# Rank-9 term carried as nine rows of a gathered list, and x loaded in place, in a two-layer graph kernel

## The chip, the cores and the metric

The kernel runs on one core of a Trainium2 chip. The metric is device time in microseconds (us) of one execution; lower is better. Times of several plain executions are given as their median, and one more execution was taken under the hardware profiler, which also records what every engine and every DMA queue did. Engines are named as in the profile: PE (TensorE matmul), PEld (its weight load), DVE (VectorE), ACT (ScalarE), POOL (GpSimd) and SP (SyncE, which here only issues DMAs).

## The reference, cut to what matters

x is (8, 2048, 128): 8 batches, 2048 nodes, 128 features. adj is a sparse symmetric-pattern 2048 x 2048 matrix in dense storage, with a full diagonal and about 18,400 entries that are not zero.

```
# layer 0
res = si[:, :, None] + sj[:, None, :] + adj * w_r + g_b      # si = x @ w_i, sj = x @ w_j
x   = layernorm(x + (res @ x) @ weight + bias)
# layer 1, five matrices of features: X, two hops of adj, and the same two again
h1  = adj^T X ;  h2 = 2 * adj^T h1 - X
x   = layernorm(x + relu([X, h1, h2, h1, h2] @ Theta1 + bias1))
```

With Y0 = x @ weight, layer 0 is `w_r * adj @ Y0` plus a term that is the same low-rank product for every node: si times the column sums of Y0, plus a row that doesn't depend on the node. For the 8 batches together this is 8 scalars per node (si) and a constant one, against 9 rows of 1024 numbers. This is the rank-9 term.

## The kernel before, in words

**Tiling.** The 2048 nodes are 16 chunks of 128. A chunk of rows is a tile of 128 partitions x 1024 (8 batches x 128 features), 512 KB in fp32. A result chunk is accumulated in two PSUM banks, one per half of the batches ("both halves", `h` in 0 and 1).

**Layer 0, dense and listed chunks.** While adj and x are read (lines 326 to 346 and 688 to 703), Y0 of every chunk is computed into the tile `Y`. Result chunks 0 to 3 are computed densely: their transposed rows of adj stay in `at4`, and `full_rows` multiplies them with all 16 chunks of `Y`. Chunks 4 to 15 are computed from lists: `Y` is stored to `y0_d` in DRAM, and the rows that a chunk needs are gathered back by indirect DMAs, issued from POOL. A listed chunk takes seven gathers (`get_rows`): four lists "T", each for a group of 32 columns, two lists "H", each for 64 columns, and a third list of H for rows that touch both halves of 64 columns. Each list has up to 128 rows, one per partition. The matching coefficients stand in `rct` (three blocks of 128 columns for each chunk, `W` = 384); `get_job` gathers them into `st` and `keep_job` masks them and writes them to `rct`. `listed` multiplies coefficients with gathered rows. The 128 x 128 block on the diagonal is done by `own_rows`, whose Y0 rows are loaded by `own0` on SP's queue (chunks 4 to 7 still lie in `Y`; 8 to 15 are loaded from `y0_d` to `ring`), with a 64 KB block `rd`.

**The rank-9 term.** `si_t(c)` transposes the 37 columns of `si` for a chunk (5 for each half, 32 apart) into PSUM and ACT copies them to `sit`. `rank9(c)` multiplies them with `ub`, 5 rows for each half, in two matmuls with 5 rows of weights. This is done for every chunk, the listed ones too.

**Order of the work.** Each engine runs its instructions in the order in which the program writes them (`Tied`). The loop over listed chunks (lines 839 to 862) issues for each chunk: the gathers on POOL, one job of coefficients, `own_rows`, the own load of chunk c+2, `rank9`, `si_t` of the next chunk, the listed matmuls, `z_add` (adds x), `make_u` of chunk c-2 (transpose of the normalised rows to `x1t`, a product with theta, and a store to `u_d`), the load of x for chunk c+2, and `layernorm`. Gathered rows go round through 12 buffers, chunks 0 to 3 and 8 to 15 of `Y`. x waits in three slots of `ring` and in `spare` (two thirds of `trp`).

**Layer 1.** `hop(1)` and `hop(2)` use the same lists with adj itself (`rc`), gathering from `u_d` and `y_d`. `hop(1)` gathers T rows once chunks 0 to 13 of `u_d` are stored, and H rows once all are.

**Ahead of the loop.** On the way there (lines 777 to 836) `make_ub` builds `ub`, DVE finds the second lists in eight rounds (`rounds2`), `lists_end(1)` turns them into indices after two small matmuls, and chunks 0 to 3 are finished. A path for inputs whose lists are too long (line 962) isn't run for this input.

Of the kernel before, what the change touches and what calls it, by code (L numbers as in the profile page):

```python
# [8 lines left out]
F32 = mybir.dt.float32  # L9
I32 = mybir.dt.int32  # L10
AF = mybir.ActivationFunctionType
ALU = mybir.AluOpType
# [6 lines left out]
def kernel(  # L19
# [34 lines left out]
    HC = NT // 2 + NC  # L54
    NI = NT + HC
    PAD = 40000
    W = 3 * P
    T_ORDER = list(range(6, NC)) + [4, 5]
    NP = LR + NC - LT
# [39 lines left out]
    def flat(t):  # L99
        return t.rearrange("p b f -> p (b f)")  # L100
# [28 lines left out]
    dve.memset(epst, EPS)  # L129
    ones = const.tile([P, P], F32)  # L130
    dve.memset(ones, 1.0)
    e5 = const.tile([1, 5], F32)
    dve.memset(e5, 0.0)
    dve.memset(e5[:, 4:5], 1.0)
    sel = const.tile([P, 8], F32)
    dve.tensor_add(sel, ident[:, 0:8], ident[:, 32:40])
    dve.tensor_add(sel, sel, ident[:, 64:72])
    dve.tensor_add(sel, sel, ident[:, 96:104])
    sel5 = const.tile([P, 4, 5], F32)
    dve.memset(sel5, 0.0)  # L140
    for i in range(4):
        dve.tensor_copy(sel5[:, i, i:i + 1], sel[:, 0:1])
        dve.tensor_copy(sel5[:, i, 4:5], sel[:, 1 + i:2 + i])
    numi = const.tile([P, NC], I32)
    pool.iota(numi, pattern=[[P, NC]], base=1, channel_multiplier=1)
    num = const.tile([P, NC], F32)
    dve.tensor_copy(num, numi)
    coli = const.tile([P, NI], I32)
    pool.iota(coli[:, 0:NT], pattern=[[1, NC], [0, QT]], base=0, channel_multiplier=0)
    pool.iota(coli[:, NT:NT + 2 * NC], pattern=[[1, NC], [0, 2]], base=0, channel_multiplier=0)  # L150
# [9 lines left out]
    idr = const.tile([P, NI], I32)  # L160
    has = const.tile([P, NI], F32)
    over = const.tile([1, 1], I32)
    si = const.tile([P, NC, 37], F32)
    dve.memset(si, 0.0)
    for h in range(2):
        dve.memset(si[:, :, 32 * h + 4:32 * h + 5], 1.0)
    sraw = const.tile([P, NC, B, 2], F32)
    s1 = const.tile([P, NC, 2, 8], F32)
    dve.memset(s1, 0.0)
# [41 lines left out]
            sp.dma_start(out=rr_d[c - ND][:, 1, :], in_=adj[:, c * P:(c + 1) * P])  # L211

    def load_z(c):
        zs[c] = load_x(c, [ring[:, 3], ring[:, 4], ring[:, 5], spare][(c - 2) % 4])

    def pump():
        while todo:
# [67 lines left out]
    def s_rows(c0):  # L285
        c4 = slice(c0, c0 + 4)
        act.activation(
            s1[:, c4, :, 1:5], sraw[:, c4, :, 0].rearrange("p c (h i) -> p c h i", h=2),
            AF.Identity, bias=gb,
        )  # L290
        for h in range(2):
            act.copy(si[:, c4, 32 * h:32 * h + 4], sraw[:, c4, h * HB:(h + 1) * HB, 1])

    pcs = bank[4:6]

# [9 lines left out]
                    tile_position=(0, 32 * j),  # L305
                )

    LAST = list(range(ND)) + list(range(8, NC)) + list(range(4, 8))
    js_first = [X_ORDER[0]] * 2 + [LAST[0]] * (ND - 2)

    def full_rows(c, accs, js):
# [156 lines left out]
    def lists_end(part):  # L468
        b = bank[6 + part]
        if part == 0:  # L470
            lo, hi = 0, NT
            for r in range(2):
                pe.matmul(
                    b[64 * r:64 * r + 64, 0:NT], lists, ident[:, 64 * r:64 * r + 64], start=True,
                    stop=True, skip_group_check=True, tile_position=(0, 64 * r),
                )
        else:
            lo, hi = NT, NI
            for r in range(2):
# [66 lines left out]
    def keep_job():  # L546
        what, c = jobs[kept[0]]
        s = staged(kept[0])
        kept[0] += 1
        m = 2 if c >= ND else 1  # L550
        hc = has[:, columns(c, what)[0]:columns(c, what)[0] + QT]
        for k in range(m):
            if m == 1 or k == 1:
                to = rc[:, c * W:(c + 1) * W]
            else:
                to = rct[:, (c - ND) * W:(c - ND + 1) * W]
            of = s[:, k * P:]
            if what == "T":
                if m == 2:
                    dve.tensor_mul(  # L560
                        to[:, 0:P].rearrange("p (t f) -> p t f", t=QT),
                        strided(of, QT, m * P + TW, TW), hc[:, :, None].to_broadcast([P, QT, TW]),
                    )
                    continue
                for t in range(QT):
                    at = t * (P + TW)
                    dve.tensor_scalar(
                        to[:, TW * t:TW * t + TW], of[:, at:at + TW], hc[:, t:t + 1], None,
                        op0=ALU.mult,
                    )  # L570
# [12 lines left out]
    def make_ub():  # L583
        cs = [trp[:, h].rearrange("p i f -> p (i f)") for h in range(2)]
        for h in range(2):
            act.copy(cs[h], pcs[h])
        pu = bank[4]
        for h in range(2):
            pe.matmul(
                pu[32 * h:32 * h + 5], e5, b0row.rearrange("p i f -> p (i f)"), start=True,  # L590
                stop=False, skip_group_check=True, tile_position=(0, 32 * h),
            )
        for i in range(4):
            s = slice(i * P, (i + 1) * P)
            for h in range(2):
                pe.matmul(
                    pu[32 * h:32 * h + 5, s], sel5[:, i, :], cs[h][:, s], start=False, stop=(i == 3),
                    skip_group_check=True, tile_position=(0, 32 * h),
                )
# [7 lines left out]
    def si_t(c):  # L607
        b = bank[turns[turn[0] % len(turns)]][0:37, 0:P]
        turn[0] += 1
        pe.transpose(b, si[:, c, :], ident)  # L610
        sits[c] = small.tile([37, P], F32, name=f"sit{c}", tag="sit")
        act.copy(sits[c], b)

    def rank9(c, accs):
        sit = sits.pop(c)
        for h in range(2):
            pe.matmul(
                accs[h], sit[32 * h:32 * h + 5], ub[32 * h:32 * h + 5].rearrange("p i f -> p (i f)"),
                start=False, stop=(c < ND), skip_group_check=True, tile_position=(32 * h, 0),
            )  # L620

    def z_add(accs, xr):
# [172 lines left out]
    rounds2([7])  # L795
# [43 lines left out]
    for c in range(ND, NC):  # L839
# [9 lines left out]
        own_rows(0, c, accs, True)  # L849
        if c + 2 < NC:  # L850
            own0(c + 2)
        rank9(c, accs)
        if c + 1 < NC:
            si_t(c + 1)
        listed(0, c, accs, "T")
        listed(0, c, accs, "H")
        z_add(accs, zs[c])
        for n in [c - 2] if c < 14 else [12, 13] if c == 14 else [14]:
            make_u(n, zs[n], x1t[n], u_of[n])
        if c + 2 < NC:  # L860
            load_z(c + 2)
        layernorm(zs[c], f"0_{c}")


# [170 lines left out]
```

## Time and profile before

| what | value |
|---|---|
| median of 3 executions (lowest, highest) | 850.22 us (850.05, 854.02) |
| the profiled execution, whole / its span | 818.08 us / 816.3 us |
| mean granted TensorE clock | 0.971 |
| PE busy / DVE / ACT / POOL | 732.8 / 394.7 / 192.7 / 445.2 us |
| gathers of Y0 and second-hop rows, 196 | 212.0 us of POOL, 1081 ns each |
| gathers of first-hop rows, 112 | 111.8 us of POOL |
| gathers of coefficients to `st`, 84 | 90.3 us of POOL |
| rank-9 matmuls, 64 records | 20.1 us of PE |
| transposes of `si`, 16 | 4.7 us of PE |
| own Y0 and second-hop rows to `ring`, 11 loads of 512 KB on SP | median 23.2 us from issue to landing |

The profile gives, for each group of instructions, busy time, the mean of one in nanoseconds, and what ended the idle time ahead of it. One fp32 matmul shows as two records. "DMA share" is the mean busy share of the 16 DMA engines. A line number in the profile is that of a helper here (L72) for nearly all instructions, so groups are told apart by tile names: `bank<-ub,sit` is the rank-9 term, `bank<-ident,si` its transpose, `Y<-y_d,idx` a gather of rows (the profile writes y_d for `y0_d` too), `st<-rr_d,idx` a gather of coefficients, `ring<-y_d` an own load. SPq lines are the issue of a DMA on SP's queue.

### The profile page before, as it was taken

The numbers are of one execution on the slowest core, as the hardware profiler recorded it, in microseconds if no ns is written. First come the engines' busy times: TensorE is split into PE (matmuls) and PEld (weight loads), VectorE is DVE, ScalarE is ACT, GpSimd is POOL, SyncE is SP. The second block draws the span as 40 slices with busy tenths as digits, with TensorE's granted clock in tenths as the row PEclk, the third lists the DMA queues.
The fourth block names the chain that finished last, engine by engine and source line by source line (L and its number), as shares of the span: only waits on it lengthen the run. The fifth ranks groups of instructions, "written<-read, shape, count | busy, mean of one in ns | idle before, by whom it ended". The sixth has DMA issues, their size and how long they took to land.

```text
span 816.3 us, 10067 instructions
## 1 busy us (share of the span) xinstructions
PE 732.8 (90%) x3554; PEld 364.9 (45%) x3554; DVE 394.7 (48%) x591; ACT 192.7 (24%) x439; POOL 445.2 (55%) x432
## 2 busy tenths in 40 slices
PE   4999999997999998988798888898899999999992
PEld 4666566642644343434345243333344454444441
DVE  4664876578341655555533000000100377777775
ACT  3757554321200332313222000000000011111101
POOL 1000000477747876776344677776774777776740
PEclk9999999997999999999899899999999999999997
DMA  8999999999326799999969799899999799999982
GB/s 264 296 314 316 352 292 295 314 398 347 119 89 223 244 346 368 341 344 367 356 224 344 246 364 360 314 365 346 339 372 357 252 343 357 370 385 389 363 299 68
DMA packets 165299, 253.90 MB, mean 311 GB/s; under 512 B 17255, under 2 KB 118020, under 8 KB 163192
## 3 DMA queue, kind: packets, MB, share of 16 engines
q0 software_dynamic: 49280, 146.52, 49.7%
q1 hardware_dynamic: 93200, 81.01, 31.1%
q10 hardware_dynamic: 22760, 25.63, 8.9%
q8 instruction: 30, 0.49, 0.2%
q14 instruction: 29, 0.24, 0.1%
HBM read 234.82 MB, written 58.72 MB: 360 GB/s over the span
## 4 chain that ended last, share of the span: by engine, by line
PE 52%; DMA 29%; issue 6%; ACT 6%; DVE 3%; POOL 2%; ACTq 0%; POOLq 0%; SPq 0%; DVEq 0%
PE bank L72 52%; DMA Y<-u_d,idx 12%; DMA Y<-y_d,idx 8%; DMA st<-rr_d,idx 2%; DMA rd<-rr_d 2%; ACT Y L72 2%; DMA ring<-in_x_dram 2%; POOL Y L72 1%; ACT rct L72 1%; ACT trp L72 1%; DMA trp<-in_adj_dram,idr 1%; DVE s L72 1%; DVE ring L72 1%; ACT at L72 1%; DVE st L72 1%
## 5 line engine op out<-in xcount | busy, mean ns | idle before, releaser
L72 POOL DMA_INDIRECT Y<-y_d,idx x196 | 212.0, 1081 | 93.2 <-PE bank L72 38.0
L72 PE MATMUL bank<-Y,rc 128*32 128x512 f32 (+2 forms) x896 | 219.7, 618 | 21.3 <-DMA Y<-u_d,idx 19.1
L72 POOL DMA_INDIRECT st<-rr_d,idx x84 | 90.3, 1075 | 183.5 <-DVE rown L72 148.3
L72 POOL DMA_INDIRECT Y<-u_d,idx x112 | 111.8, 999 | 53.9 <-issue 29.9
L72 PEld LDWEIGHTS bank<-Y,rc 128*32 128x32 f32 (+2 forms) x896 | 58.6, 130 | 179.3 <-issue 99.5
L72 PE MATMUL bank<-Y,at 128*128 128x512 f32 x256 | 115.2, 601 | 0.0
L72 PE MATMUL bank<-Y,rct 128*32 128x512 f32 (+2 forms) x336 | 77.3, 625 | 8.5 <-DMA Y<-y_d,idx 8.5
L72 DVE TENSOR_REDUCE s<-sq 128x4 f32<-128x512 f32 x64 | 43.9, 686 | 58.0 <-ACT sq L72 58.0
L72 PEld LDWEIGHTS bank<-Y,at 128*128 128x128 f32 x256 | 47.8, 193 | 53.6 <-issue 53.4
L72 DVE COPY ring<-bank 128x512 f32<-128x512 f32 x10 | 6.9, 692 | 110.1 <-PE bank L72 110.1
L72 ACT ACTIVATE sq<-ring 128x512 f32<-128x512 f32 x44 | 27.7, 630 | 129.5 <-DVE ring L72 109.7
L72 PE MATMUL bank<-ring,rd 128*128 128x512 f32 x108 | 51.5, 599 | 5.7 <-DMA rd<-rr_d 4.1
L72 PE MATMUL bank<-ident,rc 128*128 128x128 f32 (+2 forms) x302 | 45.0, 297 | 12.6 <-DMA rc<-in_adj_dram 6.6
L72 PE MATMUL bank<-th,at 128*128 128x128 f32 x384 | 49.2, 283 | 1.9 <-ACT at L72 1.9
L72 PEld LDWEIGHTS bank<-th,at 128*128 128x128 f32 x384 | 46.8, 197 | 6.7 <-ACT at L72 3.8
L72 DVE TENSOR_TENSOR ring<-bank,ring 128x512 f32<-128x512 f32 x26 | 17.3, 688 | 66.0 <-PE bank L72 60.8
L72 DVE TENSOR_REDUCE st<-rc 128x64 f32<-128x2048 f32 x16 | 36.5, 2283 | 25.7 <-DMA rc<-in_adj_dram 25.7
L72 ACT COPY ring<-bank 128x512 f32<-128x512 f32 x34 | 19.9, 586 | 122.5 <-PE bank L72 112.9
L72 PEld LDWEIGHTS bank<-Y,rct 128*32 128x32 f32 (+2 forms) x336 | 20.8, 130 | 57.3 <-issue 32.4
L72 PEld LDWEIGHTS bank<-ident,rc 128*128 128x128 f32 (+2 forms) x302 | 33.8, 150 | 25.5 <-issue 9.1
L72 PE MATMUL bank<-wx,trp 128*128 128x130 f32 x256 | 36.9, 288 | 4.3 <-ACT trp L72 2.2
L72 PE MATMUL bank<-ident,ring 128*128 128x128 f32 x232 | 32.5, 282 | 6.4 <-DMA ring<-in_x_dram 2.8
(142 smaller groups left out, 789.1 us busy)
## 6 DMA issues: line engine op xcount, KB each, us to landing
rc<-in_adj_dram SPq DMA_DIRECT2D x16, 1024.0 KB, 10.9
ring<-in_x_dram SPq DMA_DIRECT2D x25, 512.0 KB, 8.5
rr_d<-in_adj_dram SPq DMA_DIRECT2D x12, 1024.0 KB, 10.8
rr_d<-Y SPq DMA_DIRECT2D x8, 1024.0 KB, 9.0
y_d<-Y SPq DMA_DIRECT2D x16, 512.0 KB, 10.6
u_d<-ring ACTq DMA_DIRECT2D x12, 512.0 KB, 7.0
ring<-y_d SPq DMA_DIRECT2D x11, 512.0 KB, 23.2
ring<-u_d SPq DMA_DIRECT2D x10, 512.0 KB, 3.9
```

The source lines that it names most:

```text
L72: return lambda *a, **k: tc.keep_in_program_order(f(*a, **k))
```

## The change

For listed chunks the separate rank-9 step goes away. Its nine coefficient rows and nine value rows take the last nine places (partitions 119 to 127) of the third H list. `ub_rows` writes the value rows once, into two buffers `C0` that from now on hold only third lists in layer 0; `si_rows` writes the coefficient rows of all 12 chunks into `rct`; `keep_job` adds the masked coefficients on top of them for partitions 96 to 127; `lists_end(1)` marks those nine places as not used, so that the gathers leave them alone. To get nine rows and not ten, the two halves share one constant row, which changes the constants `e5` and `sel5` and the layout of `si`; `si_t`, still used for chunks 0 to 3, becomes two small matmuls and two copies.

x of a chunk is loaded to where its `x1t` will be, and layernorm and transpose then work in that place. This frees ring slots and `spare`: the gather buffers of layer 0 become 10 (`Y` 0 to 3 and 12 to 15, `ring` 0 and 1) and the two of `C0` (`ring` 5 and `spare`). Own Y0 rows of chunks 8 to 11 now stay in `Y` too and aren't loaded. The x loads move: chunks 4 and 5 after layernorm of chunk 2, 6 and 7 after `rank9(3)`, the others in the loop at the chunks that a small table names.

```diff
+    LC = 96
+    R9 = 23
-    e5 = const.tile([1, 5], F32)
+    e5 = const.tile([1, 2, 5], F32)
...
+    eb = const.tile([37, P - LC], F32)
...
-    sel5 = const.tile([P, 4, 5], F32)
+    sel5 = const.tile([P, 2, 4, 5], F32)
     dve.memset(sel5, 0.0)
     for i in range(4):
-        dve.tensor_copy(sel5[:, i, i:i + 1], sel[:, 0:1])
-        dve.tensor_copy(sel5[:, i, 4:5], sel[:, 1 + i:2 + i])
+        for h in range(2):
+            dve.tensor_copy(sel5[:, h, i, h + i:h + i + 1], sel[:, 0:1])
+            dve.tensor_copy(sel5[:, h, i, 4 - 4 * h:5 - 4 * h], sel[:, 1 + i:2 + i])
...
+    free = const.tile([P, 1], F32)
+    dve.tensor_scalar(free, num[:, 0:1], float(LC + R9), None, op0=ALU.is_le)
...
-    si = const.tile([P, NC, 37], F32)
+    si = const.tile([P, NC, P - LC], F32)
...
     def load_z(c):
-        zs[c] = load_x(c, [ring[:, 3], ring[:, 4], ring[:, 5], spare][(c - 2) % 4])
+        zs[c] = load_x(c, x1t[c])
...
-    LAST = list(range(ND)) + list(range(8, NC)) + list(range(4, 8))
+    LAST = list(range(ND)) + list(range(12, NC)) + list(range(4, 12))
...
+        if part:
+            dve.tensor_scalar(pl[:, 2 * NC:], pl[:, 2 * NC:], free, None, op0=ALU.mult)
...
+            lo = LC if m == 2 and k == 0 else P
             dve.tensor_scalar(
-                to[:, 2 * P:3 * P], of[:, 2 * m * P:2 * m * P + P], has[:, i:i + 1], None,
+                to[0:lo, 2 * P:3 * P], of[0:lo, 2 * m * P:2 * m * P + P], has[0:lo, i:i + 1], None,
                 op0=ALU.mult,
             )
+            if lo < P:
+                dve.scalar_tensor_tensor(
+                    to[lo:, 2 * P:3 * P], of[lo:, 2 * m * P:2 * m * P + P], has[lo:, i:i + 1],
+                    to[lo:, 2 * P:3 * P], op0=ALU.mult, op1=ALU.add,
+                )
...
     def si_t(c):
...
-        pe.transpose(b, si[:, c, :], ident)
+        for h in range(2):
+            pe.matmul(
+                b[32 * h:32 * h + 5], si[:, c, R9 + 4 * h:R9 + 4 * h + 5], ident, start=True,
+                stop=True, skip_group_check=True, tile_position=(0, 32 * h),
+            )
         sits[c] = small.tile([37, P], F32, name=f"sit{c}", tag="sit")
-        act.copy(sits[c], b)
+        for h in range(2):
+            act.copy(sits[c][32 * h:32 * h + 5], b[32 * h:32 * h + 5])
+
+    def si_rows(c0):
+        b = by4(bank[turns[turn[0] % len(turns)]])[LC:]
+        turn[0] += 1
+        for i in range(4):
+            pe.matmul(
+                b[:, i, :], si[:, c0 + i, :], ident, start=True, stop=True, skip_group_check=True,
+                tile_position=(0, LC),
+            )
+        r = rct.rearrange("p (c w) -> p c w", w=W)
+        act.copy(r[LC:, c0 - ND:c0 - ND + 4, 2 * P:3 * P], b)
+
+    def ub_rows(gs):
+        for h in range(2):
+            pe.matmul(
+                bank[4 + h][LC:], eb[32 * h:32 * h + 5],
+                ub[32 * h:32 * h + 5].rearrange("p i f -> p (i f)"), start=True, stop=True,
+                skip_group_check=True, tile_position=(32 * h, LC),
+            )
+        for g in gs:
+            for h in range(2):
+                act.copy(g[LC:, h * 512:(h + 1) * 512], bank[4 + h][LC:])
...
-    load_z(4)
-    NG = 12
-    G = [flat(Y[:, n]) for n in LAST[:NG]]
-    g_at = [0]
+    G0 = [flat(Y[:, n]) for n in LAST[:8]] + [flat(ring[:, n]) for n in range(2)]
+    C0 = [flat(ring[:, 5]), flat(spare)]
+    G1 = [flat(Y[:, n]) for n in list(range(4)) + list(range(8, NC))]
+    g_at = [0, 0]
...
-            g = G[g_at[0] % NG]
-            g_at[0] += 1
+            if i == 0 and what == "H" and n == 2:
+                g = C0[c % 2]
+            else:
+                of = G1 if i else G0
+                g = of[g_at[i > 0] % len(of)]
+                g_at[i > 0] += 1
...
     def own0(c):
-        load_own(0, y0_d, c, Y[:, c] if c < 8 else ring[:, c % 2], c < 8)
+        load_own(0, y0_d, c, Y[:, c] if c < 12 else ring[:, 3 + c % 2], c < 12)
...
-    load_z(ND + 1)
...
     rank9(0, acc0)
     rank9(1, acc1)
+    ub_rows(C0)
+    for c in range(ND, NC, 4):
+        si_rows(c)
...
     layernorm(zs[2], "0_2")
+    load_z(4)
+    load_z(5)
...
     rank9(3, acc3)
-    si_t(ND)
+    load_z(6)
+    load_z(7)
...
-        rank9(c, accs)
-        if c + 1 < NC:
-            si_t(c + 1)
         listed(0, c, accs, "T")
         listed(0, c, accs, "H")
         z_add(accs, zs[c])
...
-        if c + 2 < NC:
-            load_z(c + 2)
+        for n in {7: [11, 12], 10: [13], 12: [14], 14: [15]}.get(c, [c + 4] if c < 7 else []):
+            load_z(n)
```

More of the change, by code (lines that the diff above doesn't have):

```diff
@@ L131 @@
     dve.memset(ones, 1.0)
-    e5 = const.tile([1, 5], F32)
+    e5 = const.tile([1, 2, 5], F32)
     dve.memset(e5, 0.0)
-    dve.memset(e5[:, 4:5], 1.0)
+    dve.memset(e5[:, 0, 4:5], 1.0)
+    dve.memset(e5[:, 1, 0:1], 1.0)
+    eb = const.tile([37, P - LC], F32)
+    dve.memset(eb, 0.0)
+    for h in range(2):
+        dve.tensor_copy(
+            eb[32 * h:32 * h + 5, R9 + 4 * h:R9 + 4 * h + 5],
+            ident[32 * h:32 * h + 5, 32 * h:32 * h + 5],
+        )
     sel = const.tile([P, 8], F32)
@@ L162 @@
     over = const.tile([1, 1], I32)
-    si = const.tile([P, NC, 37], F32)
+    si = const.tile([P, NC, P - LC], F32)
     dve.memset(si, 0.0)
-    for h in range(2):
-        dve.memset(si[:, :, 32 * h + 4:32 * h + 5], 1.0)
+    dve.memset(si[:, :, R9 + 4:R9 + 5], 1.0)
     sraw = const.tile([P, NC, B, 2], F32)
@@ L291, in s_rows @@
         for h in range(2):
-            act.copy(si[:, c4, 32 * h:32 * h + 4], sraw[:, c4, h * HB:(h + 1) * HB, 1])
+            act.copy(
+                si[:, c4, R9 + 5 * h:R9 + 5 * h + 4], sraw[:, c4, h * HB:(h + 1) * HB, 1]
+            )
     pcs = bank[4:6]
@@ L589, in make_ub @@
             pe.matmul(
-                pu[32 * h:32 * h + 5], e5, b0row.rearrange("p i f -> p (i f)"), start=True,
+                pu[32 * h:32 * h + 5], e5[:, h, :], b0row.rearrange("p i f -> p (i f)"), start=True,
                 stop=False, skip_group_check=True, tile_position=(0, 32 * h),
@@ L596, in make_ub @@
                 pe.matmul(
-                    pu[32 * h:32 * h + 5, s], sel5[:, i, :], cs[h][:, s], start=False, stop=(i == 3),
+                    pu[32 * h:32 * h + 5, s], sel5[:, h, i, :], cs[h][:, s], start=False, stop=(i == 3),
                     skip_group_check=True, tile_position=(0, 32 * h),
@@ L609, in si_t @@
         turn[0] += 1
-        pe.transpose(b, si[:, c, :], ident)
-        sits[c] = small.tile([37, P], F32, name=f"sit{c}", tag="sit")
-        act.copy(sits[c], b)
+        for h in range(2):
[3 more added lines that the diff above has]
+            )
+        sits[c] = small.tile([37, P], F32, name=f"sit{c}", tag="sit")
+        for h in range(2):
[7 more added lines that the diff above has]
+                tile_position=(0, LC),
+            )
+        r = rct.rearrange("p (c w) -> p c w", w=W)
[6 more added lines that the diff above has]
+                skip_group_check=True, tile_position=(32 * h, LC),
+            )
+        for g in gs:
+            for h in range(2):
+                act.copy(g[LC:, h * 512:(h + 1) * 512], bank[4 + h][LC:])
     def rank9(c, accs):
@@ L618, in rank9 @@
                 accs[h], sit[32 * h:32 * h + 5], ub[32 * h:32 * h + 5].rearrange("p i f -> p (i f)"),
-                start=False, stop=(c < ND), skip_group_check=True, tile_position=(32 * h, 0),
+                start=False, stop=True, skip_group_check=True, tile_position=(32 * h, 0),
             )
```

## The prediction

> **What bounds the kernel now.** I read the page first, then stage by stage. The chain that ended last gives PE 52% and DMA 29%; its line by names is
>
> ```profile
> PE bank L72 52%; DMA Y<-u_d,idx 12%; DMA Y<-y_d,idx 8%; DMA st<-rr_d,idx 2%; DMA rd<-rr_d 2%; ACT Y L72 2%; DMA ring<-in_x_dram 2%; POOL Y L72 1%; ACT rct L72 1%; ACT trp L72 1%; DMA trp<-in_adj_dram,idr 1%; DVE s L72 1%; DVE ring L72 1%; ACT at L72 1%; DVE st L72 1%
> ```
>
> So no single engine rules. The change acts on layer 0's listed chunks, from about 262 us to 438, and on the work just ahead. The busy time by stretches there (PE, PEld, DVE, ACT, POOL, then clock, DMA share, GB/s):
>
> ```profile
> 272.00:322.00 50.00, 44.99 (x228) 20.21 (x230) 30.27 (x52) 15.23 (x31) 37.66 (x36) 1.00 0.96 338
> 322.00:382.00 60.00, 54.76 (x262) 24.61 (x258) 30.81 (x53) 16.18 (x33) 43.40 (x43) 1.00 0.99 352
> 382.00:402.00 20.00, 13.90 (x78) 7.33 (x77) 10.98 (x18) 5.95 (x12) 10.17 (x11) 1.00 0.99 353
> 402.00:440.00 38.00, 36.08 (x192) 17.84 (x193) 17.39 (x27) 12.65 (x24) 16.58 (x16) 0.91 0.82 288
> ```
>
> From 272 to 402 the DMA engines are full (0.96 to 0.99), and PE has idle time. The timeline of POOL adds a third limit: a gather is issued every 1.30 us (0.99 busy, 0.30 idle that nothing releases), e.g.
>
> ```profile
> 350.59 0.99 POOL L72 DMA_INDIRECT Y<-y_d,idx  x1 [0.30 <-DMA Y<-y_d,idx]
> 351.88 0.99 POOL L72 DMA_INDIRECT Y<-y_d,idx  x1 [0.30 <-issue]
> ```
>
> From 239.55 to 359.68 I count 86 gathers: 86 x 1.295 = 111.4 of 120.1 us. POOL's queue is 93% full there. After 359.68 it holds no coefficient gathers, runs ahead and stops for buffers. PE's own timeline in a chunk:
>
> ```profile
> 287.63 1.88 PE L72 MATMUL bank<-Y,rd 128*128 128x512 f32 x4
> 289.44 1.13 PE L72 MATMUL bank<-ub,sit 5*128 5x512 f32 x4
> 290.50 0.30 PE L72 MATMUL bank<-ident,si 128*37 128x128 f32 x1
> 290.73 2.93 PE L72 MATMUL bank<-Y,rct 128*32 128x512 f32 x18
> ```
>
> The rank-9 pair holds PE from 289.44 to 290.50 = 1.06 us, the transpose to 290.73 = 0.23. Own rows of chunks 4 to 15 start at 262.1, 273.9, 287.6, 302.0, 313.8, 328.6, 342.4, 355.3, 370.2, 386.0, 402.1 and 420.9; layer 1's first own rows at 434.3. The shortest period, 11.8, has no wait; most have 13.7 to 15.8. The late ones are made by SP's queue, which stands still on own loads and passes `rd` on late:
>
> ```profile
> 372.12 10.37 SPq L72 DMA_DIRECT2D ring<-y_d  x1
> 382.54 1.18 SPq L72 DMA_DIRECT2D rd<-rr_d  x1
> 402.08 2.49 PE L72 MATMUL bank<-ring,rd 128*128 128x512 f32 x4 [4.07 <-DMA rd<-rr_d]
> ```
>
> **What the Trainium skill says.** "DMA: Bandwidth & Descriptors", section "Where 436 GB/s comes from": for transfers between HBM and SBUF the HBM side binds at about 358 GB/s. The trace agrees: 352 to 353 GB/s at share 0.99. Same page, "Queues, rings and completion order": each DMA engine goes round-robin between the queues that have work, a packet at a time. It fits SP's own loads, 23.2 us to landing beside the gathers of POOL's queue. "TensorE: Matmul & The Clock Gate", "Part 1: The HAM clock gate": the clock is half after an idle window and full after about 3.4 us of activity. The trace agrees: granted clock 0.50 in 186 to 192 and in 405 to 410, after sparse PE work. "TensorEngine Tiling (Array Packing)", "Tiling Modes": different tiles of the array run in parallel; the pair of 5-row matmuls shows it (1.06 us, against 1.82 for two full ones).
>
> **The change part by part**, against the profiled execution (818.08 us, span 816.3). The median of the runs shown is 850.22, 32 us more, which the profile doesn't explain; I carry the difference over unscaled.
>
> *Start.* 14 more small DVE instructions at 0.07 (8 copies `sel<-sel` took 0.58) = 1.0 us. DVE waits 0.43 us for the first rows of adj and then 3.5; that hides it. Without cover it costs 1.0. Taken: 0.
>
> *Ahead of the loop, 182 to 205.* Removed: nothing. The wider `si_t` adds ACT copies (2 x 0.21) and about 0.1 of PE before `rank9(0)`: 0.5. Behind `rank9(1)` PE gets `ub_rows` and `si_rows` before the two small matmuls of `lists_end(1)`. The cover is this wait:
>
> ```profile
> 184.41 3.33 PE L72 MATMUL bank<-ub,sit 5*128 5x512 f32 x8 [1.20 <-ACT sit L72]
> 191.20 0.46 PE L72 MATMUL bank<-ident,lists 96*64 96x48 f32 x4 [3.46 <-DVE lists L72]
> 204.06 1.09 PE L72 MATMUL bank<-ident,ring 128*128 128x128 f32 x8 [1.87 <-DVE ring L72]
> ```
>
> `ub_rows` by the nearest row (`ub,sit`): 1.06 at full clock, 1.67 as in the first line. `si_rows`: 12 matmuls of 128 columns; eight of that size (`th,at`) take 2.05, or 3.67 at half clock: 3.1 or 5.5. Sum with 0.5: 4.7 or 7.7, minus the cover 3.46: 1.2 or 4.2. The third group of `si_rows` also waits for a bank behind four ACT copies (4 x 0.59) and one of its own, which keeps the low end from being reached. I take 3.5, bounds 1 to 5. It isn't lost in PE's next wait: `lists_end(1)` on DVE, the two `z_add` and layernorm of chunk 0 stand behind it, and PE waits for those at 204.06. From there to 262 PE is 98% busy, so the delay is handed on. The masking instruction adds 0.2 (nearest: `has<-bank`, 0.22). `si_t(2)` and `si_t(3)` add 0.7, `si_t(4)` removed gives 0.2. Together **+4.2**.
>
> *Loop, PE.* Gone: 12 x 1.06 + 11 x 0.23 = 15.2 us of PE. It counts only where PE sets the end.
>
> *Loop, DMA.* Four own loads less (4 x 0.524 MB) and x of chunks 6 and 7 moved from 272 and 286 to about 262 (two loads; the DMA share is 0.51 from 265 to 275): 3.15 MB out of the full stretch, at 352 GB/s **9.0 us**. x of 4 and 5 move from 186 to 236, where the share is 0.14 to 0.43: 0. They stand on SP ahead of `rd` of chunks 4 and 5, needed only at 262.
>
> *Loop, POOL.* No gather less. Until the first T gather of chunk 12 (359.68) at most 120.1 - 111.4 = 8.8 us can be had, of which I see 3.5 as waits on PE, DMA and DVE over 0.3 (0.72, 0.45, 1.50, 1.72 are the four largest, less 0.3 each); the rest are gathers of 1.7 to 1.9 us, which the change doesn't touch. Taken: **-3.5**, bounds 0 to -8.
>
> *Loop, tail.* From 359.68 to 434.3 are 74.6 us. To be had: the rank-9 step of chunks 12 to 15 (4 x 1.3 = 5.2), waits on `rd`, own rows and gathers (4.1 + 1.6 + 1.1 = 6.8), half clock after 402 (about 3): 15. DMA stays the limit for its part: 9.0 less the 3.5 already gained = 5.5, and after 410, where the share falls to 0.5, PE's 1.3 comes on top. **-7**, bounds -3 to -14.
>
> *keep_job.* 12 more DVE instructions of 0.28 (`rct<-st,has`), hidden, DVE being half busy; POOL's coefficient gathers wait for DVE now and then: **+0.3** (to 2).
>
> *Way into layer 1.* `ring` 0 and 1 now hold T rows of chunk 15, so `hop(1)`'s first own loads wait on SP until these are used (425.6 before, own rows needed at 434.3, landing takes 3.9): 0; bound 2. The first T gathers go to `Y` 0 and 1, which H rows of chunk 15 hold until about 0.9 us later than the wait that now ends at 425.39. Their matmul starts at 436.09 without a wait, the last gather being issued at 429.28 and landing 6.0 later. `make_u(15)` stands behind it, and its store lets all H gathers go:
>
> ```profile
> 425.39 0.99 POOL L72 DMA_INDIRECT Y<-u_d,idx  x1 [6.88 <-issue]
> 436.09 1.92 PE L72 MATMUL bank<-Y,rc 128*32 128x512 f32 x16
> 438.34 1.09 PE L72 MATMUL bank<-ident,ring 128*128 128x128 f32 x8 [0.33 <-DVE ring L72]
> ```
>
> **+0.7**, bounds 0 to 2.5. x of chunk 15 is loaded a chunk later: issued when H of chunk 14 is done (414), landing after 8.5, needed at 428.7: 0.
>
> Sum: 4.2 - 3.5 - 7 + 0.3 + 0.7 = **-5.3 us**, so 812.8 in the profile and **844.9** for the median.
>
> **Rivals.**
> *PE sets the loop.* Then all 15.2 us of PE come, with waits of the late chunks on top of the ahead-of-loop cost: 4.2 - 17 + 0.7 = -12, 838. For it: PE is 90% busy. Against it: DMA share 0.99.
> *POOL's queue sets the loop to the end, and the setup is dear (the other side).* If gathers go on at 1.30 us and the transfers saved only lower the DMA share, the loop gains PE's last 1.3 and no more, while half clock makes the setup 5 + 0.7. Then 5.7 + 0.3 + 0.7 - 1.3 = +5.4: 855.6. It ends slower as soon as the loop gives less than 5.2. For it: the 93% above. Against it: POOL stops for buffers after 378 (4.46 and 10.61 us at 391 and 411).
> *The gains cancel.* Setup at 5.9, loop at -7: about 850. The third list's nine places being needed by the input would send the kernel into the long path, hundreds of us more; by counting the input, no second half of a third list has over 53 of the 55 places left, so I give it 0.01.
>
> **How the numbers follow.** Forecast case (-10 to -2) 0.45, PE case (-16 to -10) 0.22, cancelling (-2 to +3) 0.17, slower 0.16. The forecast's own range is 840 to 848. Leaving out the ends gives 836 to 855. A change of 0.5% (4.25 us) is about what this measurement can tell from none. Faster by more: PE case whole and two thirds of the forecast, with a little lost for spread: 0.55. Slower by more: 0.15. Within: 0.30.
>
> **What would show it.** Right: no `ub,sit` in listed chunks, own periods of 12.5 to 13.5, `lists_end(1)`'s matmuls 3 to 4 us later than 191.2, the first gathers of chunk 12 at about 360, DMA share under 0.97 in the middle of the loop, `ring<-y_d` seven instead of eleven and issued in under 5 us. Wrong: gathers still 1.30 apart up to chunk 15, PE idle longer on gathers (POOL sets it); or periods near 10.5 (PE sets it); or a wait of several us ahead of the first T rows of layer 1.

## The result: 0.8% slower beside the times shown, 0.8% faster at another time

Beside the kernel before, the changed kernel took 861.14 us (854.36 to 872.41, 22 executions) against 852.83 us (849.01 to 870.88): ratio 1.0078, 95% interval [1.0053, 1.0102]. The forecast was 844.9 us and faster.

One fact is needed to read every other number. **The kernel before has two levels of time**, about 850 us in some sessions and about 811 us in others, on chips of one kind and once on the same chip half an hour apart. Within each session below all plain executions are of one level. All kernels that are compared below ran in the same session, beside the kernel before. The change stands on different sides of 1 at the two levels (ratios leave out executions over 1.5% above the fastest of the same kernel, medians do not, so a ratio is not always the quotient of the medians):

| session | kernel before, median us | changed kernel | ratio, 95% interval |
|---|---|---|---|
| first | 852.83 | 861.14 | 1.0078 [1.0053, 1.0102] |
| second | 847.73 | 855.27 | 1.0113 [1.0039, 1.0188] |
| fourth | 811.65 | 804.53 | 0.9917 [0.9886, 0.9948] |
| fifth | 810.69 | 805.32 | 0.9913 [0.9890, 0.9935] |

The profile that the prediction was worked from (818.08 us) is of the shorter level, at its upper end, and the median that it was put on (850.22) is of the longer.

**The profile after**, of an execution of 861.55 us (span 859.7). Its chain by names, and its busy times over the stretches of the loop that answer to those shown of before (columns: PE, PEld, DVE, ACT, POOL, clock, DMA share, GB/s):

```profile
PE bank L74 63%; DMA Y<-u_d,idx 5%; DMA ring<-in_x_dram 2%; DMA Y<-y_d,idx 2%; ACT Y L74 2%; DMA ring<-y_d,idx 2%; POOL Y L74 1%; ACT rct L74 1%; ACT trp L74 1%; ACT at L74 1%; DVE s L74 1%; DMA y_d<-st 1%; DVE st L74 1%; ACT sq L74 1%
```

```profile
301.00:351.00 50.00, 44.55 (x228) 22.39 (x226) 34.29 (x65) 15.41 (x29) 35.08 (x34) 0.97 0.94 320
351.00:411.00 60.00, 42.54 (x213) 20.89 (x212) 28.29 (x49) 15.12 (x28) 38.77 (x37) 0.86 0.77 267
```

Where the kernel before had PE busy for 54.76 of 60 us with the DMA engines at 0.99, the changed one has 42.54 and 0.77. Neither is full: something else is waited for. (The stretch holds a stall of 15 us that is shown further down, and the two profiles are of different levels.) PE's timeline ahead of the loop:

```profile
205.94 2.35 PE L74 MATMUL bank<-ub,sit 5*128 5x512 f32 x4 [0.78 <-ACT sit L74]
208.22 1.92 PE L74 MATMUL bank<-ub,eb 5*32 5x512 f32 x4
210.07 5.33 PE L74 MATMUL bank<-ident,si 128*32 128x128 f32 x24
215.32 0.46 PE L74 MATMUL bank<-ident,lists 96*64 96x48 f32 x4
```

The new instructions (`ub,eb` and `ident,si` with 32 columns) hold PE from 208.22 to 215.32, 7.1 us at about half clock (0.54 granted from 205 to 216), and the matmuls of `lists_end(1)` follow without a wait. The 3.46 us in which PE waited for the lists in the profile of before, the cover of the prediction's setup step, is not there.

### The profile page after: what moved, and what is told of

Its sections match the earlier page's. It is cut to its first block, busy times and chain, and to the rows that moved or that the text cites. A ratio compares the mean times of both kernels' runs of the same rounds, so it can differ in the third digit from the quotient of the medians.

```text
span 859.7 us, 10035 instructions
## 1 busy us (share of the span) xinstructions
PE 738.1 (86%) x3534; PEld 374.4 (44%) x3534; DVE 399.4 (46%) x616; ACT 195.3 (23%) x438; POOL 442.0 (51%) x432
## 4 chain that ended last, share of the span: by engine, by line
PE 63%; DMA 13%; issue 8%; ACT 6%; another core or an unknown queue 5%; DVE 2%; POOL 1%; ACTq 0%; POOLq 0%; SPq 0%; DVEq 0%
PE bank L74 63%; DMA Y<-u_d,idx 5%; DMA ring<-in_x_dram 2%; DMA Y<-y_d,idx 2%; ACT Y L74 2%; DMA ring<-y_d,idx 2%; POOL Y L74 1%; ACT rct L74 1%; ACT trp L74 1%; ACT at L74 1%; DVE s L74 1%; DMA y_d<-st 1%; DVE st L74 1%; ACT sq L74 1%
## 5 line engine op out<-in xcount | busy, mean ns | idle before, releaser
L74 PE MATMUL bank<-Y,rc 128*32 128x512 f32 (+2 forms) x896 | 225.4, 616 | 28.3 <-issue 14.2
L74 POOL DMA_INDIRECT Y<-y_d,idx x170 | 184.1, 1083 | 87.9 <-issue 41.1
L74 PE MATMUL bank<-th,at 128*128 128x128 f32 x384 | 53.1, 296 | 19.8 <-issue 16.6
L74 ACT COPY ring<-bank 128x512 f32<-128x512 f32 (+1 forms) x36 | 20.9, 586 | 168.6 <-PE bank L74 90.0
L74 PE MATMUL bank<-Y,rct 128*32 128x512 f32 (+1 forms) x232 | 44.9, 601 | 0.1
L74 PE MATMUL bank<-ring,rd 128*128 128x512 f32 x92 | 43.5, 593 | 1.3 <-issue 1.1
L74 ACT ACTIVATE sq<-ring 128x512 f32<-128x512 f32 x26 | 16.4, 630 | 115.7 <-issue 53.0
L74 PEld LDWEIGHTS bank<-wx,trp 128*128 128x128 f32 x256 | 32.8, 199 | 21.3 <-issue 13.1
L74 POOL DMA_INDIRECT trp<-in_adj_dram,idr x28 | 28.0, 999 | 21.9 <-DVE rc L74 14.3
L74 ACT COPY trp<-bank 128x512 f32<-128x512 f32 (+1 forms) x38 | 21.4, 587 | 64.7 <-PE bank L74 57.5
```

Of the source, the lines that this page charges most:

```text
L74: return lambda *a, **k: tc.keep_in_program_order(f(*a, **k))
```

## Experiments

Ratios are to the kernel before in the same session.

**Both kernels again (second session), unchanged.**

> The kernel before, unchanged, profiled again. Its first profiled execution took 818.08 us, 31 us less than its fastest plain one (849.01), so that profile may not stand for the times. Theory 'odd profile': this one takes 848 to 858 us, and shows waits of several us in the stretch of layer 0 that the first profile did not have; the comparison of the two first profiles (+41.6 us of span) is then mostly an accident of the executions. Theory 'real': about 818 again, and the 41 us are the change's.

> The changed kernel, unchanged, profiled again: the first profile of it has stalls of 17 us (361 to 378) and of 5 us (166 to 177). If they belong to the change, they are at the same places again; if they are accidents of an execution, they are gone or elsewhere, and the steady parts remain: chunk periods of 10.5 to 11.5 us in layer 0's loop, and the two small matmuls of the second lists at least 8 us later after the candidates' transposes than before (26.3 us before, 36.9 in the first profile after). Ratio to before 1.005 to 1.010.

Measured: before 842.49 us in its profiled execution (median of the session 847.73), short of the 848 to 858 of 'odd profile' and far from the 818 of 'real'; changed 1.0113 [1.0039, 1.0188], a little above what was expected. The changed kernel's stall of 361 to 378 is not at its place again (there is one of 7.66 us ahead of 349.77); that of 166 to 177 is, and the kernel before has it here too. The profile of before at this level has no cover either:

```profile
203.99 3.78 PE L72 MATMUL bank<-ub,sit 5*128 5x512 f32 x8 [1.62 <-ACT sit L72]
207.70 0.46 PE L72 MATMUL bank<-ident,lists 96*64 96x48 f32 x4
```

It is late from the second candidates on. PE transposes them at 172.75, ACT copies at 181.39, and DVE, which then makes the lists in eight rounds, starts at 183.11 after 23.88 us of idle time, where in the first profile it was 167.64 and 8.93:

```profile
172.75 3.41 PE L72 MATMUL bank<-ident,rc 128*96 128x128 f32 x16
181.39 1.08 ACT L72 COPY rc<-bank 96x512 f32<-96x512 f32 x2
183.11 1.36 DVE L72 MAX8 lists<-rc 96x8 f32<-96x1152 f32 x1 [23.88 <-ACT rc L72]
```

From DVE's first round to the lists' matmuls it is 24.6 us here and 29.9 in the changed kernel (182.26 to 212.15): the setup costs 5.3 us. Own rows of chunk 4 and the first ones of layer 1, in the kernel before and in the changed one:

```profile
277.21 1.88 PE L72 MATMUL bank<-Y,rd 128*128 128x512 f32 x4
443.68 1.88 PE L72 MATMUL bank<-ring,rd 128*128 128x512 f32 x4
283.95 1.98 PE L74 MATMUL bank<-Y,rd 128*128 128x512 f32 x4
446.46 1.88 PE L74 MATMUL bank<-ring,rd 128*128 128x512 f32 x4
```

At own rows of chunk 4 the changed kernel is 6.7 us later, at layer 1's first own rows 2.8, at its second 6.1 (462.82 against 456.75), at the end 6.1 (spans 846.8 and 840.7). So in these two profiles the loop gains 4.0 us (162.5 against 166.5), the first chunk of layer 1 loses 3.3 of them again, and the loss arises ahead of the loop. The medians differ by 7.5 us.

**The two halves of the change, each alone (second session).** `p1_rank`: rank-9 rows as changed; x, own rows and load order as before, `C0` in `Y` 14 and 15, and

```
+    C0 = [flat(Y[:, 14]), flat(Y[:, 15])]
     full_rows(3, acc3, LAST[:8])
+    ub_rows(C0)
```

> The rank-9 rows alone: x, own rows and their loads as in the kernel before; the two buffers for third lists are chunks 14 and 15 of Y, filled by ub_rows after the first half of full_rows(3) instead of ahead of the second lists; si_rows stays where the change has it. Theory 'setup': the rank-9 part costs ahead of the loop (si_rows, wider si_t) and gains in it; without ub_rows in the gap the setup is 2 to 4 us dearer than before, the loop 6 to 12 faster: ratio 0.990 to 0.998. Theory 'rank-9 rows cost': the ratio is 1.005 or more, and the slow-down is theirs.

`p2_place`: x in place, own rows of chunks 8 to 11 in `Y`, loads as changed; `rank9` and `si_t` in the loop as before, and

```
+    G0 = [flat(Y[:, n]) for n in LAST[:8]] + [flat(ring[:, n]) for n in (0, 1, 5)] + [flat(spare)]
```

> x in place of x1t, own rows of chunks 8 to 11 kept in Y, the new order of the dense rows and the moved loads alone; rank-9 term by its own matmuls as before; twelve gather buffers in turn. By the prediction this takes 3.15 MB out of the full stretch of DMA: theory 'DMA' says 0.985 to 0.995. Theory 'placement costs' (the first dense and listed chunks wait for x or for buffers, or the way into layer 1 is longer): 1.005 or more, and the changed kernel's loss is from this part.

Measured: `p1_rank` 860.74 us, 1.015 [1.0093, 1.0208]; `p2_place` 847.46, 0.9967 [0.9936, 0.9999]. The loss belongs to the rank-9 rows, and the first theory for them fell. `p2_place` lies between its two theories; its interval just stays under 1, but with all its executions its median is only 0.3 us under that of the kernel before, so a gain at this level is not shown. The two profiles also show the setup with and without. `p2_place` has none of it, and its lists' matmuls come 24.6 us after DVE's first round (181.91), as in the kernel before; `p1_rank` has `si_rows` there, and they come 27.4 us after it (182.62):

```profile
206.52 0.46 PE L72 MATMUL bank<-ident,lists 96*64 96x48 f32 x4
210.06 0.32 PE L74 MATMUL bank<-ident,lists 96*64 96x48 f32 x4
```

Own rows of chunk 4 come at 275.84 and 284.51.

**Leaving the rank-9 step out, and the setup off or moved (third session, 811 us).** `e1_no_rank` is the kernel before without

```
-        rank9(c, accs)
-        if c + 1 < NC:
-            si_t(c + 1)
```

> The kernel before with the rank-9 matmuls and the transposes of si of the twelve listed chunks left out and nothing in their place (so the rank-9 term is missing from these chunks): 15.2 us of PE less in the loop, 12 x 1.06 + 11 x 0.23, no setup and no other buffers. Theory 'PE does not set the loop' (the loop is paced by gathered rows and x that land late, so freed PE time turns into waiting): ratio to the kernel before 0.995 to 1.001. Rival 'PE's time counts and the change loses it again elsewhere': 0.982 to 0.988.

`e2_place_no_rank` takes the same lines out of `p2_place`.

> The placement part alone (x in place of X1^T, own rows of chunks 8 to 11 in place; measured at 0.9967 with the rank-9 step) with the rank-9 step of the listed chunks left out as well, so the term is missing there. It is what the whole change could give if its setup cost nothing. Theory 'PE does not set the loop': 0.992 to 0.998, no more than 0.003 under the placement part. Rival 'with fewer transfers PE becomes the bound, and its 15 us count': 0.979 to 0.986.

`e3_no_setup` is the changed kernel with

```
-    ub_rows(C0)
-    for c in range(ND, NC, 4):
-        si_rows(c)
-            lo = LC if m == 2 and k == 0 else P
+            lo = P
```

> The changed kernel without ub_rows and si_rows and with the coefficients masked by one instruction as before (the rank-9 term is missing from the listed chunks); buffers, order, constants, the wider si_t as changed. Theory 'setup': the 5.3 to 6.7 us that PE was later at own rows of chunk 4 go away, ratio to the kernel before 1.000 to 1.006 where the changed kernel had 1.0113. Rival 'the loop itself loses (two buffers kept for third lists, twelve more DVE instructions)': 1.008 or more for the buffers.

`e4_early` is the changed kernel with the setup moved:

```
+            for c in range(ND, NC, 4):
+                si_rows(c)
             candidates2()
...
-    full_rows(3, acc3, LAST[:8])
+    full_rows(3, acc3, LAST[:4])
+    ub_rows(C0)
+    full_rows(3, acc3, LAST[4:8])
```

> The changed kernel, whole term computed, with its setup moved off the path: si_rows ahead of the transposes of the second candidates, where PE stood idle for 2.8 and 6.2 us (167.6 and 175.0 in the changed kernel's second profile), and ub_rows between the matmuls of full_rows of chunk 3. Theory 'setup': si_rows fills idle time and ub_rows costs PE its 1.05 us, so 4 to 5 us come back: ratio to the kernel before 1.002 to 1.007, and lists_end(1)'s matmuls come 25 to 27 us after the last transposes of candidates (31.0 in the changed kernel). Rival 'the loop loses': 1.009 or more.

Measured beside 811.38 us: `e1_no_rank` 811.70, 0.9999 [0.9978, 1.0019]; `e2_place_no_rank` 801.32, 0.9880 [0.9849, 0.9911]; `e3_no_setup` 803.90, 0.9898 [0.9868, 0.9928]; `e4_early` 806.83, 0.9936 [0.9901, 0.9970]. The first of these is the plainest reading of the study: 15.2 us of PE taken out of a loop in which PE is 90% busy, and the time doesn't move. Where the time went stands in the pages of before and of `e1_no_rank`, in the group of the listed matmuls (busy us, mean ns of one, then us of waiting):

```profile
L72 PE MATMUL bank<-Y,rct 128*32 128x512 f32 (+2 forms) x336 | 77.3, 625 | 8.5 <-DMA Y<-y_d,idx 8.5
L72 PE MATMUL bank<-Y,rct 128*32 128x512 f32 (+2 forms) x336 | 88.0, 618 | 14.7 <-DMA Y<-y_d,idx 14.6
```

They wait 6.2 us more for gathered rows and are spread over 10.7 us more, though one of them is no longer: fewer run side by side, which fits lists that land one after the other. Together that is 16.9 us, about what was taken out. `e2_place_no_rank` fell between its theory and its rival. The two setup kernels did better than either theory's numbers, which were set for the longer level and don't hold here, so the changed kernel and its halves were measured at this level too.

**The changed kernel, its halves and the moved setup once more (fourth session, 811 us).**

> The changed kernel once more, since the kernel before took 848 us beside the first four runs and 811 us beside the next four, and both profiles of the changed kernel are from executions of the longer kind. Theory 'level': what the change is worth depends on which level the chip is at. If the kernel before takes about 811 us here, PE waits 3.5 us and more for the lists on DVE ahead of lists_end(1), as it does in every profile of that level, the setup is half hidden, and the ratio is 0.991 to 0.997; at about 848 us it is 1.007 to 1.016 as before. Rival 'the change is slower at either level': 1.005 or more here too.

> The rank-9 rows alone (x and own rows where they were), measured at 1.015 beside 848 us. Theory 'level': at 811 us 0.998 to 1.004 (leaving the rank-9 step out altogether gave 0.9999 there, so its place in the gathered list can't win, and the setup is half hidden); at 848 us 1.010 to 1.020. Rival 'the rows lose in the loop at either level': 1.008 or more.

> The placement alone, measured at 0.9967 beside 848 us. Theory 'transfers and PE only count together' (beside 811 us leaving out the rank-9 step gave 0.9999, and with the placement as well 0.988): 0.995 to 1.000 here. Rival 'the placement gives all of it': 0.987 to 0.991 at 811 us.

> The changed kernel with its setup moved (si_rows ahead of the second candidates' transposes, ub_rows into full_rows of chunk 3), measured at 0.9936 beside 811 us. At 811 us again 0.992 to 0.996, and within 0.003 of the changed kernel, whose setup is half hidden there; at 848 us, where the changed kernel lost 5 to 7 us ahead of the loop, 1.002 to 1.008 and at least 0.003 under the changed kernel. Rival 'the place of the setup doesn't matter': no difference from the changed kernel at 848 us.

Measured beside 811.65 us: changed 804.53, 0.9917 [0.9886, 0.9948]; rows alone 814.50, 1.0037 [1.0019, 1.0056]; placement alone 800.45, **0.9857** [0.9825, 0.9888]; setup moved 807.00, 0.9948 [0.9926, 0.9971]. "Level" held for the changed kernel and the rows. For the placement its rival was right, and its 0.987 to 0.991 not quite enough: the placement gives all of the gain, and the rows take a part of it back, 4.1 us by the medians. The setup and the adding instructions are about 2 of these (fifth session); where the rest is lost was not found. The moved setup is 0.0031 above the changed kernel, just outside the expected 0.003. At this level the placement alone beats both kernels; at the longer one it is shown to beat the changed kernel only. With it in place, leaving out the rank-9 step gains nothing either (0.9880 against 0.9857).

The changed kernel's profile here (span 802.7) shows the cover at work:

```profile
183.44 2.26 PE L74 MATMUL bank<-ub,sit 5*128 5x512 f32 x8 [1.11 <-ACT sit L74]
185.63 1.17 PE L74 MATMUL bank<-ub,eb 5*32 5x512 f32 x4
186.74 4.30 PE L74 MATMUL bank<-ident,si 128*32 128x128 f32 x24
190.97 0.32 PE L74 MATMUL bank<-ident,lists 96*64 96x48 f32 x4
```

5.3 us of new work stand between `rank9` and the lists, and the lists' matmuls come at 190.97, where before had them at 191.20. In `e4_early` `si_rows` stands ahead of the candidates, where PE was idle only at the longer level:

```profile
165.04 2.81 PE L74 MATMUL bank<-ident,si 128*32 128x128 f32 x24
168.51 2.24 PE L74 MATMUL bank<-ident,rc 128*96 128x128 f32 x18 [0.67 <-ACT rct L74]
171.31 1.36 DVE L74 MAX8 lists<-rc 96x8 f32<-96x1152 f32 x1 [12.58 <-ACT rc L74]
```

It pushes DVE's first round to 171.31 (166.68 in the changed kernel), and DVE's eight rounds are what the lists wait for: the lists' matmuls come at 194.85, own rows of chunk 4 at 267.95 against 264.05. Moved out from behind the cover, the work cost 2.5 us more here (807.00 against 804.53).

**Once more, for the cause at the longer level (fifth session; the chip was at 811 us).**

> The changed kernel beside the two that take its setup away or move it. At about 848 us for the kernel before: 1.007 to 1.016 as measured twice there; at about 811 us: 0.989 to 0.995 as measured once.

> The changed kernel with its setup moved. At 848 us, theory 'no cover' (there PE comes to the matmuls of lists_end(1) without a wait, so the whole setup of 5.3 us is paid; moved, si_rows falls into PE's idle time ahead of the second candidates): 0.004 to 0.007 under the changed kernel. Rival 'stalls in the loop make the loss': within 0.003 of it. At 811 us: 0.002 to 0.004 above the changed kernel, as measured.

> The changed kernel without si_rows, ub_rows and the adding instruction of keep_job (the rank-9 term is missing from the listed chunks). At 848 us, theory 'no cover': 0.006 to 0.009 under the changed kernel, that is 1.000 to 1.006 against the kernel before. Rival 'stalls': within 0.004 of the changed kernel. At 811 us: 0.988 to 0.992 as measured.

> The kernel before without the rank-9 step of the listed chunks (term missing there). At 811 us 0.9999 was measured. At 848 us, theory 'PE does not set the loop at either level': 0.996 to 1.002. Rival 'where transfers and signals are late, a shorter PE chain helps': 0.985 to 0.992.

Measured beside 810.69 us: changed 805.32, 0.9913 [0.9890, 0.9935]; `e4` 807.74, 0.9957 [0.9937, 0.9976]; `e3` 803.19, 0.9883 [0.9836, 0.9930]; `e1` 812.37, 1.0005 [0.9986, 1.0025]. A repeat of what the shorter level gives, with `e4` 0.0044 above the changed kernel where 0.002 to 0.004 was expected; what the expectations say of the longer level was not tested. Here setup and adding instructions together cost 805.32 - 803.19 = 2.1 us, with ratios whose intervals overlap. A further session for `e3` met 811 us again:

> The changed kernel without si_rows, ub_rows and the adding instruction of keep_job (the rank-9 term is missing from the listed chunks), once more, at another time. If the kernel before takes about 848 us: theory 'no cover' 1.000 to 1.006, where the changed kernel had 1.0078 and 1.0113; rival 'stalls' 1.007 or more. If it takes about 811 us: 0.987 to 0.991 as measured twice.

Measured 803.71 beside 810.48 us, 0.9883 [0.9838, 0.9929].

**Which part of the placement pays.** In the profile of the changed kernel four gathers of layer 0 go out long before the loop (POOL's timeline at the shorter level):

```profile
198.12 1.79 POOL L74 DMA_INDIRECT ring<-y_d,idx  x1 [0.30 <-DVE s L74]
200.22 0.99 POOL L74 DMA_INDIRECT trp<-y_d,idx  x1 [0.30 <-issue]
217.97 1.00 POOL L74 DMA_INDIRECT ring<-y_d,idx  x1 [0.31 <-issue]
228.41 1.00 POOL L74 DMA_INDIRECT ring<-y_d,idx  x1 [0.30 <-issue]
```

In before the first such gather is at 239.55. These four buffers lie in `ring` and `spare`, which the dense chunks don't read, and POOL issues them ahead of coefficient gathers that the program's text writes first. So the sentence further up, that each engine runs in written order, is not true of these gathers. `e5_late` is `p2_place` with

```
     layernorm(zs[2], "0_2")
+    for g in G0[8:]:
+        dve.memset(g[:, 0:1], 0.0)
```

which holds the four back.

> The placement alone (0.9857 beside 811 us, 0.9967 beside 848), with one column of each of the four gather buffers that lie in ring and spare set to zero after layernorm of chunk 2. Their first gathers must wait for that, so they stand in POOL's queue where they stood before; in the profiles of the placement four of them are issued between 196 and 232, ahead of the loop, and in the changed kernel between 198 and 229. Theory 'lookahead' (what the placement gives is largely these four gathers, 4 x 1.295 = 5.2 us of POOL's full queue and their transfers): beside 811 us 0.990 to 0.995, and the 57th gather of Y0 rows again at 358 to 361 instead of 355. Rival 'fewer loads' (the own loads and x loads taken out of the full stretch give it all): 0.984 to 0.988. Beside 848 us: 0.997 to 1.003 by the first, 0.995 to 0.998 by the second.

Measured beside 809.80 us: 804.12, 0.9920 [0.9890, 0.9950]. Its first gather is at 238.85 again. The 57th, the first of chunk 12, is at 356.98, 2.2 us later than in the placement (354.74) and short of the 358 to 361 expected. By the times, of the placement's 11.2 us about half (5.7) remains without the early gathers: both parts pay, and neither theory was the whole. The two kernels ran in different sessions, and their intervals only just stay apart; between their profiles the loop differs by 2.4 us (157.4 against 155.0).

## Why the prediction was wrong, step by step

**The step that failed first** is the one on the times: the median is "32 us more, which the profile doesn't explain; I carry the difference over unscaled". Those 32 us were not a constant on top. They were another level, in which the waits that the sum was built on are others. At the level of the profile itself the forecast was good: -5.3 of 818.08 us is a ratio of 0.9935, and 0.9917 and 0.9913 were measured. That it came so close is in part luck: the setup cost about 2 us less than forecast and the way into layer 1 about 2 us more, and about half of the placement's gain came by gathers that start early, which the prediction did not have.

**Ahead of the loop, +4.2.** At the longer level its term was mis-sized because its cover was absent: 5.3 us at the lists, 6.7 at own rows of chunk 4, over the upper bounds of 5 for the setup and 5 + 0.7 with the small terms. At the shorter level own rows of chunk 4 come at 264.05 against 262.13, +1.9, and taking setup and adding instructions away gives 2.1: the cover was larger than 3.46, since all 5.3 us of new PE work fit ahead of the lists. That the rank-9 rows make the loss at the longer level is shown by `p1_rank` and `p2_place`. That it is their setup rests on the profiles of that level: 24.6 us to the lists without it, 27.4 with `si_rows`, 29.9 with all of it. The changed kernel with nothing but its setup gone was not run at that level.

**Loop, PE: "counts only where PE sets the end".** Right, and more so than the prediction had it. It still listed 5.2 us of the rank-9 step of chunks 12 to 15 among what the tail could give, and counted 1.3 of them in its -7. `e1_no_rank` says 0 for all twelve (0.9999 and 1.0005). The rival "PE sets the loop" (838) falls with it, at the shorter level; at the longer one the step was not left out.

**Loop, DMA: 9.0 us for 3.15 MB.** The placement gives 11.2 us at the shorter level, of which `e5_late` leaves 5.7 to the loads. So the mechanism was there, and its term was over half too large. Own loads are seven instead of eleven, and land in a median of 8.0 us instead of 23.2. But 352 GB/s is not shown to be the ceiling that the prediction took it for: the page of before has slices of the span at 385 and 389. The DMA share in the changed kernel's loop is under 0.97, as said:

```profile
285.00:335.00 50.00, 46.53 (x224) 20.87 (x223) 33.66 (x59) 14.91 (x29) 38.95 (x37) 1.00 0.96 336
335.00:385.00 50.00, 45.37 (x209) 19.63 (x208) 30.21 (x54) 13.97 (x26) 38.03 (x36) 1.00 0.96 344
```

**Loop, POOL: -3.5, "no gather less".** True of the count and not of the place: four gathers left the full queue, 4 x 1.295 = 5.2 us, a step that the prediction lacked. The 57th gather (chunk 12's first) is at 355.15 instead of 359.68, 4.5 us earlier. Sum of the loop at the shorter level: 153.8 us from own rows of chunk 4 to layer 1's, against 172.1 in the profile of before, where -10.2 was forecast. That profile flatters the gain: at 818 us it lies above its level's 811, and its loop holds a wait of 4.07 us and a spell of half clock that the profile of `e1_no_rank` (166.7 us; as a whole it takes as long as the kernel before) does not have. Against that one the loop gains 12.9.

**Way into layer 1, +0.7, bounds 0 to 2.5.** Own rows of layer 1 to the end took 384.9 us against 382.0. The sign it named, a wait ahead of the first T rows, is there, and at 1.28 + 1.48 = 2.76 us a little over the bound:

```profile
421.98 1.05 PE L74 MATMUL bank<-Y,rc 128*32 128x512 f32 x4 [1.28 <-DMA Y<-u_d,idx]
424.51 1.90 PE L74 MATMUL bank<-Y,rc 128*32 128x512 f32 x10 [1.48 <-DMA Y<-u_d,idx]
```

**The slower rival** had the deciding point right, "slower as soon as the loop gives less than 5.2": at the longer level the loop gave 4.0, and 3.3 of these were lost again on the way into layer 1. Its mechanism wasn't it. The loop there isn't paced by POOL at 1.30 us a gather; POOL waits for buffers there too, and there are stalls in which PE, DVE and ACT all stand, as here in the first profile after:

```profile
361.72 1.04 PE L74 MATMUL bank<-ident,at 128*128 128x128 f32 x8
371.07 0.69 DVE L74 TENSOR_TENSOR Y<-bank,Y 128x512 f32<-128x512 f32 x1 [7.62 <-remote]
377.42 0.59 ACT L74 COPY at<-bank 128x512 f32<-128x512 f32 x1 [16.75 <-remote]
378.06 2.08 PE L74 MATMUL bank<-th,at 128*128 128x128 f32 x8 [15.30 <-issue]
```

PE's transposes end at 362.8. ACT's copy of them, which waits for nothing but PE, starts 14.7 us later, and PE waits for ACT ("remote" stands for a releaser that the profile doesn't have; the profiles of the longer level record only about half of the semaphore events of the others, 6,073 against 11,930 in the first two, so that a releaser can be missing from the record alone). Every profile of the longer level has such stalls in the loop, with PE idle for 3 us (the unchanged kernel) to 15; at the shorter level PE's idle times of over 2 us in the loop are rare, 4.07 us at most, and end with a DMA or, once, with DVE. What makes them is open. The placement gains nothing in the loop there (167.6 us in `p2_place` against 166.5 in before). The stalls can have taken its gain; but the listed matmuls of before also wait only 2.5 us there, where it was 8.5 in the first profile, so there was less to gain. The runs don't separate the two.

## What to carry to other kernels

Before a sum is made on a profile, compare the profiled execution with the plain ones: where they differ by several per cent, the waits of the profile, and the covers that are read from them, may not exist in the executions that are counted. Work put behind a wait is free only as long as the wait is there, and work put ahead of the instruction that the wait is for was not free here: it delayed the end of the wait. In a loop that waits for transfers, taking 15 us from the busiest engine can give nothing: the time turned into waiting for the same rows. A gather that could start early because its buffer was free paid about its slot in the issuing queue.

## What was not expected of the hardware

The same program takes 811 or 848 us in sessions half an hour apart on one chip (mean granted TensorE clock of its executions about 0.977 and 0.957). Between the two profiles of the kernel before, the longer one's extra time lies ahead of the loop (15.1 us at own rows of chunk 4) and from layer 1's first own rows to the end (397.0 us against 382.0), not in the loop (166.5 against 172.1). At the longer level ACT has a copy that starts 14.7 us after the only thing that it waits for in the program was done; what holds it is open. And `e1_no_rank`: PE at 90% busy, 15.2 us of its work removed, ratio 0.9999.
